# Edge tiles of 127 rows instead of 128 in a gather-and-sum graph layer on one Trainium2 core

## The chip, the cores and the metric

The kernel runs on one core of one Trainium2 chip. The metric is the device time of one execution in microseconds (us), lower is better. The kernel before takes 1381.88 us (median of two runs, 1380.68 and 1383.08).

## What is computed

`x` has 6250 nodes of 128 float32 features; 100,000 edges carry a source node, a destination node and a type 0 or 1, and come sorted by destination. Cut to what matters, the reference is:

```
Xs     = X[src]
m_data = Xs @ W_data.T + b_data
m_ctrl = Xs @ W_control.T + b_control
msg    = where(edge_types == 0, m_data, m_ctrl)
agg    = segment_sum(msg, dst, num_segments=6250)
out    = relu(agg + (X @ W_self.T + b_self))
result = layernorm(x + out)          # over the 128 features
```

## The kernel before

Nodes are padded to 49 blocks of 128 (`NB`), taken in 7 groups of 7 blocks (`GB`, `NG`). The work has a front and a long middle.

**Front.** GpSimd loads all edges once (`e_all`, L65), SyncE's queue loads weights, biases and the transposed features (`w_sb`, `bias_sb`, `xt_sb`, L67 to L72). VectorE counts, for each of 48 block borders, how many destinations lie below it (`less`, L96); one small matmul (L99) and one instruction (L101) make of it `first`, the place in the edge list at which each block's edges begin. TensorE and VectorE make both possible messages of every node, `y` (L109, L110), and ScalarE's queue writes them to a table in DRAM in seven stores of 896 KB (L111). Then (in the code; on its queue, once `first` is there) SyncE's queue reads each block's *window* of edges: `values_load` puts the window's start into a register (L119), and one DMA (L123) brings `KT * P` = 18 x 128 edges of three int32 into `win`, as 128 rows of 54 numbers (216 bytes), one row to a partition. ScalarE's queue also loads `x_sb` (L127).

**Middle.** For each group VectorE turns windows into table rows (`idx`, L132 and L133) and into destinations relative to their block (`rel`, L181), and counts the edges that lie inside (L183, L185). For each block and each of 18 tiles, GpSimd issues one indirect DMA (L195) that gathers 128 rows of 512 bytes from the table into `msg`, VectorE builds a one-hot matrix `hot` (L199), and TensorE adds `hot`^T x `msg` to `agg` in PSUM (L201; the self term L193 opened it). When a block is complete VectorE adds bias, relu and residual (L138, L139); after seven blocks the norm (L145 to L162) and one store on SyncE's queue (L166; the last, of 106 rows, L171). At the very end the count of matched edges is compared with 100,000 (L207 to L214); only if they differ, a slow loop over all edges runs. The fullest block of these inputs has 2184 edges.

**What sets the order.** The framework schedules each engine's instructions and gives every DMA one of eight completion semaphores per kind, here called lanes: eight for DMAs issued by SyncE and ScalarE together, eight for those issued by GpSimd. A DMA waits until the previous DMA on its lane has landed. In the built program, from the eighth on, a gather so waits for the gather eight before it. The lanes of SyncE and ScalarE tie the table stores to the window loads: counting windows from 0, store 3 (of 7) waits for window 5, store 4 for window 10, store 5 for window 14, store 6 for window 18, store 7 for window 23. On VectorE's queue the `idx` work of group 0 waits for windows 0 to 6 and stands in front of the later `y` additions; the next groups' `other` (L132, up to window 27) stands in front of the first block's L138. The first gather waits for the last table stores and for `idx` of group 0 (VectorE's 73rd counted instruction). Buffers: `y` and `idx` two, `msg` four blocks, `hot` three blocks, `agg` two.

Of the kernel before, what the change touches and what calls it, by code (L numbers as in the profile page):

```python
# [9 lines left out]
F32 = mybir.dt.float32  # L10
I32 = mybir.dt.int32
# [4 lines left out]
DRAM = bass.MemoryType.DRAM  # L16

P = 128
D = 128  # features
N = 6250  # nodes  # L20
E = 100000  # edges
NB = 49  # blocks of 128 nodes, the last one padded
NP = NB * P
GB = 7  # blocks in a group: one store, one set of norms
NG = NB // GB
KT = 18  # tiles of 128 edges in a block's window
WIN = KT * P
EC = 125  # edges are cut into 125 rows of 800
EPS = 1e-05


# [1 line left out]
def kernel(  # L33
    ctx: ExitStack,
    tc: tile.TileContext,
    x: bass.AP,  # [NP, D], zero rows behind N
    xt: bass.AP,  # [D, NP], its transpose
    edges: bass.AP,  # [E, 3]: source, destination, type
    w: bass.AP,  # [D, 3 * D]: data, control and self weights, transposed
    bias: bass.AP,  # [1, 3 * D]  # L40
    out: bass.AP,  # [N, D]
):
    """out = layernorm(x + relu(sum over in-edges of (W_type x_src + b_type) + W_self x + b_self))

    Both messages of each node go to a table in DRAM, at rows 2 * node + (type != 0). Edges come
    sorted by destination, so those of a block of 128 nodes lie behind one another: a window of
    WIN edges from the block's first one (found on the chip) is gathered from the table, 128 rows
    at a time, and summed by destination with one-hot matrices on the tensor engine. An edge
    outside its block matches no column there. The edges matched are counted; if any was missed
    (a block with more edges than its window, or edges in another order), a loop over all  # L50
    edges that takes them in any order does the sums again.
    """
    nc = tc.nc

    const = ctx.enter_context(tc.tile_pool(name="const", bufs=1))
    dram = ctx.enter_context(tc.tile_pool(name="dram", bufs=1, space=DRAM))
    work = ctx.enter_context(tc.tile_pool(name="work", bufs=2))
    deep = ctx.enter_context(tc.tile_pool(name="deep", bufs=4))
# [1 line left out]
    ps_a = ctx.enter_context(tc.tile_pool(name="ps_a", bufs=2, space=PSUM))  # L60
    ps_s = ctx.enter_context(tc.tile_pool(name="ps_s", bufs=1, space=PSUM))

# [1 line left out]
    e_all = const.tile([EC, E // EC, 3], I32, name="e_all")  # L64
    nc.gpsimd.dma_start(e_all, edges.rearrange("(p k) c -> p k c", p=EC))  # L65
    w_sb = const.tile([D, 3 * D], F32, name="w_sb")
# [9 lines left out]
    x_sb = const.tile([P, NB, D], F32, name="x_sb")  # L76
    x_rows = x.rearrange("(b p) f -> p b f", p=P)

# [1 line left out]
    ones = const.tile([P, 1], F32, name="ones")  # L80
    nc.vector.memset(ones, 1.0)
    slots = const.tile([P, P], F32, name="slots")
    nc.gpsimd.iota(slots, pattern=[[1, P]], base=0, channel_multiplier=0,
                   allow_small_or_imprecise_dtypes=True)
    base = const.tile([P, NB, KT], F32, name="base")
    nc.gpsimd.iota(base, pattern=[[P, NB], [0, KT]], base=0, channel_multiplier=0,
                   allow_small_or_imprecise_dtypes=True)

# [1 line left out]
    dst_f = const.tile([EC, E // EC], F32, name="dst_f")  # L90
    nc.vector.tensor_copy(dst_f, e_all[:, :, 1])  # L91
    before = const.tile([EC, NB], F32, name="before")
# [7 lines left out]
    first = const.tile([1, NB], I32, name="first")  # L100
    nc.vector.tensor_scalar_min(first, first_ps, float(E - WIN))  # L101

# [1 line left out]
    table = dram.tile([NP, 2 * D], F32, name="table")  # L104
    for g in range(NG):
        y = work.tile([P, GB, 2 * D], F32, name="y")
# [6 lines left out]
        )  # L113
    rows = table.rearrange("n (t f) -> (n t) f", t=2)

# [1 line left out]
    win = const.tile([P, NB, KT, 3], I32, name="win")  # L117
    for b in range(NB):
        at = nc.values_load(  # L119
            first[0:1, b : b + 1], engines=(SP,), min_val=0, max_val=E - WIN,  # L120
            skip_runtime_bounds_check_because="it counts edges and is held to E - WIN",
        )
        nc.sync.dma_start(  # L123
            win[:, b, :, :], edges[ds(at, WIN), :].rearrange("(p k) c -> p k c", p=P)
        )
    for g in range(NG):
        nc.scalar.dma_start(x_sb[:, g * GB : (g + 1) * GB, :], x_rows[:, g * GB : (g + 1) * GB, :])  # L127

    def table_rows(index, source, kind, shape):
        """index = 2 * source + (kind != 0)"""  # L130
        other = work.tile(shape, I32, name="other")
        nc.vector.tensor_single_scalar(other, kind, 0.0, op=ALU.not_equal)  # L132
        nc.vector.scalar_tensor_tensor(index, source, 2.0, other, op0=ALU.mult, op1=ALU.add)  # L133

    def residual(h, agg, b):
        """h = x + relu(agg + b_self)"""
        s = work.tile([P, D], F32, name="s")
        nc.vector.tensor_add(s, agg, bias_sb[:, 2 * D :])  # L138
        nc.vector.scalar_tensor_tensor(h, s, 0.0, x_sb[:, b, :], op0=ALU.max, op1=ALU.add)  # L139

    def norm_and_store(h, g):
        mv = work.tile([P, GB, 2], F32, name="mv")
        for j in range(GB):
            st = work.tile([P, 6], F32, name="st")
            nc.vector.bn_stats(st, h[:, j, :])  # L145
            nc.vector.bn_aggr(mv[:, j, :], st)  # L146
        # One step of Newton's method behind the table's square root: 1 / root is 2 / (s + v / s).
        v = work.tile([P, GB], F32, name="v")
        nc.vector.tensor_scalar_add(v, mv[:, :, 1], EPS)  # L149
        s0 = work.tile([P, GB], F32, name="s0")  # L150
        nc.scalar.activation(s0, v, AF.Sqrt)  # L151
        r0 = work.tile([P, GB], F32, name="r0")
        nc.vector.reciprocal(r0, s0)
        q = work.tile([P, GB], F32, name="q")
        nc.vector.tensor_mul(q, v, r0)
        nc.vector.tensor_add(q, q, s0)
        rstd = work.tile([P, GB], F32, name="rstd")
        nc.vector.reciprocal(rstd, q)
        nc.vector.tensor_scalar_mul(rstd, rstd, 2.0)
        o = work.tile([P, GB, D], F32, name="o")  # L160
        for j in range(GB):
            nc.vector.tensor_scalar(o[:, j, :], h[:, j, :], mv[:, j, 0:1], rstd[:, j : j + 1],  # L162
                                    op0=ALU.subtract, op1=ALU.mult)
        n0 = g * GB * P
        full = min(GB, (N - n0) // P)
        nc.sync.dma_start(  # L166
            out[n0 : n0 + full * P, :].rearrange("(b p) f -> p b f", p=P), o[:, :full, :]
        )
        if full < GB:
            n1 = n0 + full * P  # L170
            nc.sync.dma_start(out[n1:N, :], o[: N - n1, full, :])  # L171

# [1 line left out]
    counts = const.tile([P, NG], F32, name="counts")  # L174
    for g in range(NG):
        gs = slice(g * GB, (g + 1) * GB)
        shape = [P, GB, KT]
        idx = work.tile(shape, I32, name="idx")
        table_rows(idx, win[:, gs, :, 0], win[:, gs, :, 2], shape)
        rel = work.tile(shape, F32, name="rel")  # L180
        nc.vector.tensor_sub(rel, win[:, gs, :, 1], base[:, gs, :])  # L181
        low = work.tile(shape, F32, name="low")
        nc.vector.tensor_single_scalar(low, rel, float(P), op=ALU.is_lt)  # L183
        inside = work.tile(shape, F32, name="inside")
        nc.vector.scalar_tensor_tensor(inside, rel, 0.0, low, op0=ALU.is_ge, op1=ALU.mult,  # L185
                                       accum_out=counts[:, g : g + 1])
        h = work.tile([P, GB, D], F32, name="h")
        for j in range(GB):
            b = g * GB + j
            msg = deep.tile([P, KT, D], F32, name="msg")  # L190
            hot = deep.tile([P, KT, P], F32, name="hot", bufs=3)
            agg = ps_a.tile([P, D], F32, name="agg")
            nc.tensor.matmul(agg, xt_sb[:, b, :], w_sb[:, 2 * D :], start=True, stop=False)  # L193
            for k in range(KT):
                nc.gpsimd.indirect_dma_start(  # L195
                    out=msg[:, k, :], out_offset=None, in_=rows,
                    in_offset=bass.IndirectOffsetOnAxis(ap=idx[:, j, k : k + 1], axis=0),
                )
                nc.vector.tensor_single_scalar(hot[:, k, :], slots, rel[:, j, k : k + 1],  # L199
                                               op=ALU.is_equal)  # L200
                nc.tensor.matmul(agg, hot[:, k, :], msg[:, k, :], start=False, stop=k == KT - 1)  # L201
            residual(h[:, j, :], agg, b)
        norm_and_store(h, g)

# [1 line left out]
    total_ps = ps_s.tile([1, NG], F32, name="total_ps")  # L206
    nc.tensor.matmul(total_ps, ones, counts, start=True, stop=True)  # L207
    total_f = const.tile([1, 1], F32, name="total_f")
    nc.vector.tensor_reduce(total_f, total_ps, axis=mybir.AxisListType.X, op=ALU.add)
    total = const.tile([1, 1], I32, name="total")  # L210
# [1 line left out]
    matched = nc.values_load(total[0:1, 0:1])  # L212

    with tc.If(matched != E):  # L214
        # Rows behind N take what is not to be added: an edge whose destination an earlier edge of
        # its tile has already is in that edge's sum.
        sums = dram.tile([N + P, D], F32, name="sums")
        ident = const.tile([P, P], F32, name="ident")
        make_identity(nc, ident)
# [13 lines left out]
        with tc.For_i(0, E, EC) as i:  # L233
# [16 lines left out]
            n_again = work.tile([EC, 1], F32, name="n_again")  # L250
            nc.vector.scalar_tensor_tensor(again, same, 1.0, earlier[:EC, :EC], op0=ALU.mult,
                                           op1=ALU.mult, accum_out=n_again)
            # The destination, or a spare row where it came before.
            away = work.tile([EC, 1], F32, name="away")
            nc.vector.tensor_sub(away, spare[:EC], to)
            nc.vector.scalar_tensor_tensor(away, n_again, 0.0, away, op0=ALU.is_gt, op1=ALU.mult)
# [54 lines left out]
```

## Time and profile before

| what | value |
|---|---|
| time, median of 2 runs (lowest, highest) | 1381.88 us (1380.68, 1383.08) |
| span of the profiled execution (first to last instruction) | 1220.6 us |
| time of the runs less that span (the profile lists no other time of its own execution) | 161.3 us |
| first gather starts / last gather starts | 98.12 us / 1206.64 us |
| GpSimd busy | 843.7 us, 69% of the span |
| TensorE matmul busy | 747.0 us, 61% |
| VectorE busy | 305.0 us, 25% |
| DMA moved | 77.32 MB in 55893 packets, mean 63 GB/s |
| granted TensorE clock, mean | 0.540 |

How to read it: PE, PEld, DVE, ACT, POOL and SP are TensorE matmul, TensorE weight load, VectorE, ScalarE, GpSimd and SyncE; a q behind the name (SPq, ACTq) is that engine's DMA-issuing queue. A group of the profile names line, engine, operation and tiles (out<-in), shapes and count, then busy time and the mean length of one in ns, then the idle time ahead of it and what ended most of it. In the DMA lists, the last number is the median time from issue to landing. "issue" is time in which an engine waited for nothing that the profile shows. A POOL bar of an indirect DMA ends before its data has landed.

### The profile page before, as it was taken

Reading aid. Unit: us, or ns where it says so; the run is one execution under the profiler, and the core shown is the slowest. Engines: PE = TensorE matmul, PEld = TensorE weight load, DVE = VectorE, ACT = ScalarE, POOL = GpSimd, SP = SyncE. Lnnn points to the kernel's source line nnn. Section 1 sums busy time; section 2 is a strip of 40 time slices with the busy share of each in tenths; the row PEclk is TensorE's granted clock in tenths of the full one; section 3 lists DMA queues with packets and bytes.
Section 4 is the critical chain, followed back from the end, with each engine's and each line's share of the span. In section 5 each row is a group of like instructions: output and inputs, shape, how many; then the busy total and the mean of one; then the engine's idle time right before and its main releaser. Section 6 shows DMA issues by size and latency. Waiting matters only on the chain.

```text
span 1220.6 us, 6620 instructions
## 1 busy us (share of the span) xinstructions
PE 747.0 (61%) x1964; PEld 478.7 (39%) x1964; DVE 305.0 (25%) x1362; ACT 2.7 (0%) x8; POOL 843.7 (69%) x889
## 2 busy tenths in 40 slices
PE   1094666666666666666666666666666666666664
PEld 0042444444444344444444444444444444444442
DVE  4982211221212312212213113113122112212101
ACT  0000000000000000000000000000000000000000
POOL 0005777777777777777777777777777777777774
PEclk9995555555555555555555555555555555555555
DMA  8063121122212211121222212222122211221121
GB/s 263 0 200 95 52 54 52 52 67 54 52 52 52 69 52 52 52 54 52 67 54 53 52 52 67 54 52 53 52 67 54 52 52 52 68 53 52 52 54 49
DMA packets 55893, 77.32 MB, mean 63 GB/s; under 512 B 21669, under 2 KB 40719, under 8 KB 55727
## 3 DMA queue, kind: packets, MB, share of 16 engines
q0 software_dynamic: 28368, 59.06, 18.6%
q1 hardware_dynamic: 14716, 8.16, 2.5%
q10 hardware_dynamic: 12768, 9.63, 2.4%
q8 instruction: 16, 0.26, 0.1%
q14 instruction: 25, 0.20, 0.1%
HBM read 67.17 MB, written 9.62 MB: 63 GB/s over the span
## 4 chain that ended last, share of the span: by engine, by line
POOL 63%; issue 23%; DMA 5%; DVE 5%; PE 2%; POOLq 0%; SPq 0%; DVEq 0%; ACT 0%; ACTq 0%
POOL msg L195 63%; DMA msg<-table,idx 4%; DVE less L96 4%; PE y_ps L109 2%; DMA xt_sb<-in_xt 1%; DVE hot L199 1%; DVE y L110 1%; PE agg L201 0%; DVE o L162 0%; POOLq L307 0%; SPq L67 0%; SPq L69 0%; POOLq L195 0%; PE first_ps L99 0%; DVE other L132 0%
## 5 line engine op out<-in xcount | busy, mean ns | idle before, releaser
L195 POOL DMA_INDIRECT msg<-table,idx x882 | 840.9, 953 | 362.6 <-issue 259.5
L201 PE MATMUL agg<-msg,hot 128*128 128x128 f32 x1764 | 695.2, 500 | 403.0 <-DMA msg<-table,idx 400.7
L201 PEld LDWEIGHTS agg<-msg,hot 128*128 128x128 f32 x1764 | 441.0, 311 | 656.5 <-DMA msg<-table,idx 656.2
L138 DVE TENSOR_TENSOR s<-agg,bias_sb 128x128 f32<-128x128 f32 x49 | 14.3, 292 | 790.4 <-PE agg L201 790.4
L199 DVE TENSOR_SCALAR hot<-slots,rel 128x128 f32<-128x128 f32 x882 | 189.0, 292 | 0.0
L96 DVE TENSOR_SCALAR_CACHE_REDUCE less<-dst_f 125x800 f32<-125x800 f32 x48 | 43.6, 980 | 0.0
L109 PE MATMUL y_ps<-w_sb,xt_sb 128*128 128x256 f32 x98 | 31.4, 449 | 18.5 <-DMA xt_sb<-in_xt 16.8
L193 PE MATMUL agg<-w_sb,xt_sb 128*128 128x128 f32 x98 | 31.2, 423 | 0.0
L109 PEld LDWEIGHTS y_ps<-w_sb,xt_sb 128*128 128x128 f32 x98 | 16.5, 207 | 31.9 <-issue 16.8
L193 PEld LDWEIGHTS agg<-w_sb,xt_sb 128*128 128x128 f32 x98 | 27.0, 333 | 0.6 <-DVE s L138 0.3
L99 PE MATMUL first_ps<-before,ones 125*1 125x49 f32 x2 | 0.3, 260 | 41.5 <-DVE less L96 41.5
L133 DVE SCALAR_TENSOR_TENSOR idx<-win,other 128x126 int32<-128x126 int32 x7 | 2.3, 324 | 88.0 <-DMA msg<-table,idx 88.0
L110 DVE TENSOR_TENSOR y<-y_ps,bias_sb 128x256 f32<-128x256 f32 x49 | 20.5, 424 | 5.0 <-PE y_ps L109 3.8
L99 PEld LDWEIGHTS first_ps<-before,ones 125*1 125x1 f32 x2 | 0.1, 80 | 41.8 <-DVE less L96 41.8
L139 DVE SCALAR_TENSOR_TENSOR h<-s,x_sb 128x128 f32<-128x128 f32 x49 | 14.5, 295 | 0.1
L145 DVE BATCH_NORM_STATS2 st<-h 128x6 f32<-128x128 f32 x49 | 13.7, 280 | 0.1
L162 DVE TENSOR_SCALAR o<-h,mv,rstd 128x128 f32<-128x128 f32 x49 | 13.5, 363 | 0.0
L146 DVE BATCH_NORM_AGGREGATE mv<-st 128x2 f32<-128x6 f32 x49 | 8.6, 176 | 0.9
L91 DVE CAST dst_f<-e_all 125x800 f32<-125x800 int32 x1 | 0.7, 693 | 15.5 <-DMA e_all<-in_edges 15.5
L151 ACT ACTIVATE s<-v 128x7 f32<-128x7 f32 x7 | 1.5, 208 | 1115.5 <-DVE v L149 1115.5
L96 DVE DVE_READ_ACCUMULATOR less<-dst_f 125x1 f32 x48 | 3.9, 82 | 0.0
L181 DVE TENSOR_TENSOR rel<-win,base 128x126 f32<-128x126 int32 x7 | 2.1, 305 | 0.0
(25 smaller groups left out, 19.2 us busy)
## 6 DMA issues: line engine op xcount, KB each, us to landing
msg<-table,idx POOLq DMA_INDIRECT x882, 2.5
table<-y ACTq DMA_DIRECT2D x7, 896.0 KB, 4.2
x_sb<-in_x ACTq DMA_DIRECT2D x7, 448.0 KB, 14.6
xt_sb<-in_xt SPq DMA_DIRECT2D x7, 448.0 KB, 10.4
out<-o SPq DMA_DIRECT2D x6, 448.0 KB, 3.0
win<-in_edges SPq DMA_DIRECT2D x49, 27.0 KB, 1.9
e_all<-in_edges POOLq DMA_DIRECT2D x1, 1171.9 KB, 15.2
out<-o SPq DMA_DIRECT2D x1, 384.0 KB, 3.4
```

The source lines that it names most:

```text
L96: nc.vector.tensor_scalar(less, dst_f, float(b * P), None, op0=ALU.is_lt, op1=ALU.add, accum_out=before[:, b : b + 1])
L109: nc.tensor.matmul(y_ps, xt_sb[:, g * GB + j, :], w_sb[:, : 2 * D], start=True, stop=True)
L110: nc.vector.tensor_add(y[:, j, :], y_ps, bias_sb[:, : 2 * D])
L138: nc.vector.tensor_add(s, agg, bias_sb[:, 2 * D :])
L139: nc.vector.scalar_tensor_tensor(h, s, 0.0, x_sb[:, b, :], op0=ALU.max, op1=ALU.add)
L145: nc.vector.bn_stats(st, h[:, j, :])
L146: nc.vector.bn_aggr(mv[:, j, :], st)
L162: nc.vector.tensor_scalar(o[:, j, :], h[:, j, :], mv[:, j, 0:1], rstd[:, j : j + 1], op0=ALU.subtract, op1=ALU.mult)
L193: nc.tensor.matmul(agg, xt_sb[:, b, :], w_sb[:, 2 * D :], start=True, stop=False)
L195: nc.gpsimd.indirect_dma_start(out=msg[:, k, :], out_offset=None, in_=rows, in_offset=bass.IndirectOffsetOnAxis(ap=idx[:, j, k : k + 1], a ...
L199: nc.vector.tensor_single_scalar(hot[:, k, :], slots, rel[:, j, k : k + 1], op=ALU.is_equal)
L201: nc.tensor.matmul(agg, hot[:, k, :], msg[:, k, :], start=False, stop=k == KT - 1)
```

## The change

A constant `R = 127` takes the place of 128 for the number of edges in a tile. Everything that has one partition per edge has 127 partitions: the window (2286 edges instead of 2304, still 18 edges to a row), `idx`, `rel`, `msg`, `hot`, and each of the 882 gathers. The number of tiles stays 18 per block, so no instruction is added or removed: on all five engines the instructions, their order and the semaphores they wait for are the same in both built programs, with 127 in the place of 128. Blocks of nodes, the message table, the norms and the stores keep 128. Comments are taken out.

```diff
 KT = 18
-WIN = KT * P
+R = 127
+WIN = KT * R
...
-    win = const.tile([P, NB, KT, 3], I32, name="win")
+    win = const.tile([R, NB, KT, 3], I32, name="win")
...
-            win[:, b, :, :], edges[ds(at, WIN), :].rearrange("(p k) c -> p k c", p=P)
+            win[:, b, :, :], edges[ds(at, WIN), :].rearrange("(p k) c -> p k c", p=R)
...
-        shape = [P, GB, KT]
+        shape = [R, GB, KT]
...
-        nc.vector.tensor_sub(rel, win[:, gs, :, 1], base[:, gs, :])
+        nc.vector.tensor_sub(rel, win[:, gs, :, 1], base[:R, gs, :])
...
-                                       accum_out=counts[:, g : g + 1])
+                                       accum_out=counts[:R, g : g + 1])
...
-            msg = deep.tile([P, KT, D], F32, name="msg")
-            hot = deep.tile([P, KT, P], F32, name="hot", bufs=3)
+            msg = deep.tile([R, KT, D], F32, name="msg")
+            hot = deep.tile([R, KT, P], F32, name="hot", bufs=3)
...
-                nc.vector.tensor_single_scalar(hot[:, k, :], slots, rel[:, j, k : k + 1],
+                nc.vector.tensor_single_scalar(hot[:, k, :], slots[:R], rel[:, j, k : k + 1],
                                                op=ALU.is_equal)
...
-    nc.tensor.matmul(total_ps, ones, counts, start=True, stop=True)
+    nc.tensor.matmul(total_ps, ones[:R], counts[:R], start=True, stop=True)
```

## The prediction, made blind

> **What bounds the kernel now.** I read the chain of waits first, then the groups by line, then the timeline around the first gather, then the DMA issues. Chain and groups:
>
> ```profile
> POOL 63%; issue 23%; DMA 5%; DVE 5%; PE 2%; POOLq 0%; SPq 0%; DVEq 0%; ACT 0%; ACTq 0%
> ...
> L195 POOL DMA_INDIRECT msg<-table,idx x882 | 840.9, 953 | 362.6 <-issue 259.5
> L201 PE MATMUL agg<-msg,hot 128*128 128x128 f32 x1764 | 695.2, 500 | 403.0 <-DMA msg<-table,idx 400.7
> ```
>
> See: the chain is GpSimd issuing gathers, with "issue" (no visible wait) between them, while TensorE waits 400.7 us for gathered rows. The first gather starts at 98.12 us and the 882nd at 1206.64 us, so the pace is 1108.5 / 881 = 1.258 us. TensorE needs about 0.80 us per tile (the timeline's two matmuls of a tile) and VectorE 0.21 us; both follow. So the time has three terms: the front up to 98.1 us, 882 x 1.258 us, and a tail of 14 us; 161.3 us lie around the span (1381.88 - 1220.6), and I leave them alone. The timeline shows what ends the front:
>
> ```profile
> 63.47 49.07 SPq L123 DMA_DIRECT2D win<-in_edges  x49
> ...
> 66.51 26.87 ACTq L111 DMA_DIRECT2D table<-y  x7
> ...
> 98.12 1.03 POOL L195 DMA_INDIRECT msg<-table,idx  x1 [94.01 <-DVE inside L185]
> 99.45 0.96 POOL L195 DMA_INDIRECT msg<-table,idx  x1 [0.30 <-issue]
> ```
>
> and the DMA issues:
>
> ```profile
> msg<-table,idx POOLq DMA_INDIRECT x882, 2.5
> table<-y ACTq DMA_DIRECT2D x7, 896.0 KB, 4.2
> ...
> win<-in_edges SPq DMA_DIRECT2D x49, 27.0 KB, 1.9
> ```
>
> See: SyncE issues a window load per 1.00 us (49.07 / 49), each landing after 1.9 us; store 7 of the table is issued at 93.0 us and lands 4.2 us later, and the gathers then start. The profile names VectorE's L185 as releaser, but the built program only waits there for `idx` of group 0 (done near 73 us), so I take the store as the real release.
>
> [...] In its packet records (size, time and duration of each DMA packet), the last store of 106 rows (divisor 2) drains as two interleaved streams, each a 512-byte row per 23.4 ns, so the divisor counts on SyncE's queue. The 125-row `e_all` load of GpSimd moved up to 20 packets per us of 601 ns each, at least 12 engines' worth, so that direct copy isn't confined to 5. No run here shows an indirect gather with an odd row count. [...]
>
> **The change part by part.** The built program has the same instructions, order and waits on all engines; only lengths can change.
>
> *Window loads (49).* 127 rows of 216 bytes would all go to one engine, always the same one. The packet records give 16 ns as the median of such a row (mean 19.7 with waits), so one load takes that engine 127 x 16 = 2.03 us, where 16 engines took 0.13 us each. The loads now queue at 2.04 us instead of 1.00 us. On the same engine lies its share of each table store: 56 rows of 1 KB at 46 ns = 2.6 us. Store 7 waits on its lane for window 23, the 24th load. That lands at 63.5 + (1.9 - 0.13) + 24 x 2.04 + 6 stores x 2.6 = 129.8 us. Store 7 was issued at 93.0 us; so it is late by 36.8 us. Its own rows on that engine alternate with queued window rows: 56 x 16 ns = 0.9 us more. First gather: 98.1 + 37.7 = 135.8 us.
>
> Is something else later still? VectorE stops at `idx` of group 0 until window 6: 63.5 + 1.8 + 7 x 2.04 + 2 x 2.6 = 84.8 us instead of 71.8 us, 13 us late. Behind it stand `y` additions and `hot`; the last `y` addition moves from 92.8 to 106 us, or some 10 us more where stores 4 to 6 wait for windows 10, 14 and 18: by about 116 us, before 129.8. VectorE's `other` for window 27 ends near 139 us; behind it L138 of block 0 is wanted only at 136 + 18 x 1.26 = 158 us. Later windows (all landed by about 185 us) serve groups that start 158 us apart. These cost nothing under that cover; at 24 ns per row (the spacing of the last store), the 24 loads cost 24 us more and the cover for L138 still nearly holds. Bounds for this term: 0 (spread) to 62 us (24 ns); I take 37.7, since packet time is what one engine can pass.
>
> *Gather, data.* 127 rows on one engine are 16 packets of up to 4096 bytes. A packet took 229 ns (median; 156 and 382 at the 5th and 95th percentile), so the last row lands 15 x 0.229 = 3.4 us later: 5.9 us instead of 2.5. The wait this meets is the lane: gather i waits for gather i-8, that is 8 x 1.258 = 10.1 us. 5.9 is under it[...]. So nothing on the pace; 3.4 us once, at the last gather, since the tail waits for it. Bounds: 0 (spread over 16) to 5.7 us (382 ns).
>
> *Gather, generation.* 127 rows instead of 128: if all 953 ns are per row, 7.4 ns x 882 = 6.6 us less; if none, 0. I take 3.3. Whether one ring is dearer or cheaper to fill than sixteen shows nowhere in this trace: 1% of the 840.9 us is 8.4 us. I take zero for it and treat it as cases below.
>
> *Compute.* Matmul contraction and the DVE tiles lose one partition of 128; [...] both engines wait anyway: 0. The fullest block, 2184 edges, fits 2286, so the slow loop stays out.
>
> Sum: 37.7 + 3.4 - 3.3 = +37.8 us. Span 1258.4, time 1381.9 + 37.8 = 1420 us (median and span are set together by the constant 161.3).
>
> **The rivals.**
>
> *A, likeliest (45%).* As summed. Own range 1405 (14 ns rows, gathers spread, full saving of 6.6) to 1450 (24 ns rows, slow gather packets).
>
> *B, generation gets dearer (22%).* [...] For it: POOL is the pace, so everything counts 882 times. Against: no row shows it. +10% is 84 us, 1504; +25% is 210 us, 1630.
>
> *C, generation gets cheaper, the other side (18%).* If much of the 953 ns is work per DMA engine[...], a gather on one ring saves some of it at L195. Against: [...]the packet records show 16 four-byte packets per gather[...]. It decides at 37.8 / 840.9 = 4.5%: more saving than that ends below the time before. At 10%: 1420 - 84 = 1336.
>
> *D, gathers in one line (6%).* [...]every gather sits on the same engine: 16 x 0.229 = 3.7 us per gather, the lane wait binds, 882 x (3.7 - 1.26) = 2150 us more, about 3570 us. The same wait decides whenever landing passes 10.1 us, 60 ns per row; the trace's 29 ns per row[...] speak against it.
>
> *E, the change doesn't do that (9%).* Windows spread over 16 engines as `e_all` did, gathers too. Then only the row less counts: 1382 - 3 = 1378 us. The two streams of the 106-row store speak against it.
>
> **How the numbers follow.** The time is A's, 1420. A measurement of this kernel tells about 2% (27.6 us) from no change: below 1354 is faster, above 1409.5 slower. Slower: four fifths of A (0.37), B (0.22), D (0.06) = 0.65. Faster: C where it saves over 8% (0.10), 0.11 with a rest. Same: the remainder of A and C, and E, 0.24. For the range I leave out D, the worst fourth of B (above 1560) and the lower half of C (below 1350): 0.06 + 0.06 + 0.09 = 0.21. So 1350 to 1560, and 1405 to 1450 for A alone.
>
> **What would show it.** In the profile after: window loads to landing well above 1.9 us, up to 14 us when seven queue; the window line of SyncE's queue about 100 us or more long; store 7 near 130 us; the first gather near 136 us; gathers to landing near 5.9 us; GpSimd's mean 947 to 953 ns; idle before L195 still "issue" 0.30 us. Wrong in A: first gather below 110 us (windows spread, or one engine passes rows faster than 16 ns), POOL's mean off by over 2% (B or C), or gathers waiting for gathers (D).

## The result and the profile after

The changed kernel takes 2660.93 us (median of two runs, 2660.41 and 2661.45) where the kernel before takes 1381.88 us: a ratio of 1.926, 95% interval 1.920 to 1.931. The forecast was 1420 us with a range up to 1560; it is missed by far. The profiled execution has a span of 2658.2 us, and its own time is 2660.4 us, so only 2.2 us lie around the span.

The kernel before runs at one of two speeds according to the chip, 1375 to 1383 us on some and 1220 to 1222 us on another, and the profile of before (span 1220.6 us) shows the second, as run 7 below confirms. So the "161.3 us" that "lie around the span" don't exist, and each experiment below is compared with runs of the kernel before on its own chip.

First the page of the changed kernel: the chain's shares by engine, then the two groups (busy us, mean ns | idle us before them and what ended most of it). Every line number is one higher than before.

```profile
POOL 79%; issue 10%; DMA 7%; DVE 2%; SPq 2%; PE 1%; POOLq 0%; DVEq 0%; ACT 0%; ACTq 0%
...
L196 POOL DMA_INDIRECT msg<-table,idx x882 | 2246.2, 2547 | 391.5 <-issue 385.7
L202 PE MATMUL agg<-msg,hot 127*128 127x128 f32 x1764 | 701.7, 501 | 1815.2 <-DMA msg<-table,idx 1815.2
```

See: the same chain as before, GpSimd issuing gathers, and the same count of them. Only the length of one has changed, from 953 to 2547 ns. TensorE's matmuls are as long as they were (501 ns) and wait 1815.2 us for rows.

The timeline around the first gather (start and length in us):

```profile
63.61 108.37 SPq L124 DMA_DIRECT2D win<-in_edges  x49
...
66.52 53.77 ACTq L112 DMA_DIRECT2D table<-y  x7
...
127.26 2.62 POOL L196 DMA_INDIRECT msg<-table,idx  x1 [123.14 <-issue]
```

See: the window loads take 108.37 us instead of 49.07 us, 2.2 us each; the last table store is issued near 120 us instead of 93; and the first gather starts at 127.26 us instead of 98.12. The gap ahead of a gather is still 0.30 us of "issue". A gather's line in the DMA issues ends with the time from issue to landing:

```profile
msg<-table,idx POOLq DMA_INDIRECT x882, 7.7
```

The span's difference, term by term: the front 127.26 - 98.12 = 29.1 us; the pace, (2639.26 - 127.26) / 881 = 2.851 us per gather instead of 1.258, so 881 x 1.593 = 1403.4 us; the tail from the start of the last gather 18.9 us instead of 14.0, so 5.0 us. 1220.6 + 29.1 + 1403.4 + 5.0 = 2658.1, the span but for rounding. Nearly all of it is the length of one instruction.

What is in those 1.6 us shows in a part of the page that I hadn't used in the forecast, the DMA queues (packets, MB, share of 16 engines). GpSimd's queue q0, first before, then after:

```profile
q0 software_dynamic: 28368, 59.06, 18.6%
```

```profile
q0 software_dynamic: 240048, 65.33, 15.4%
```

Before: 28368 = 144 (the one load of all edges) + 882 x 32, and 32 is 16 packets of eight 512-byte rows and 16 marks of four bytes. After: (240048 - 144) / 882 = 272, that is 240 packets more for the same rows. The bytes say what they are. 882 x 127 x 512 B are 57.35 MB, the load of the edges 1.20 MB, the marks 0.06 MB; 6.72 MB are left, 7620 bytes per gather, which is 15 x 127 x 4. The packet records of the trace agree: per gather they hold 15 packets of 4096 bytes and one of 3584 (127 rows, eight to a packet), 16 of four bytes, 225 of 32 bytes and 15 of 28. 225 and 15 are fifteen times the same, 15 packets of 32 bytes and one of 28, in four-byte pieces 15 x 8 + 7 = 127. The records carry no engine number, but one reading meets all these counts, and those of six other row counts below: the 127 rows are one share of a gather, and fifteen further shares of 127 four-byte fillers each go with it, as many as the one share has rows.

### The profile page after: what moved, and what is told of

The parts are those of the page before. It is cut to its first block, busy times and chain, and to the rows that moved or that the text cites. A ratio compares the mean times of both kernels' runs of the same rounds, so it can differ in the third digit from the quotient of the medians.

```text
span 2658.2 us, 6620 instructions
## 1 busy us (share of the span) xinstructions
PE 757.1 (28%) x1964; PEld 481.9 (18%) x1964; DVE 542.4 (20%) x1362; ACT 2.7 (0%) x8; POOL 2249.1 (85%) x889
## 3 DMA queue, kind: packets, MB, share of 16 engines
q0 software_dynamic: 240048, 65.33, 15.4%
q1 hardware_dynamic: 13932, 8.15, 1.1%
## 4 chain that ended last, share of the span: by engine, by line
POOL 79%; issue 10%; DMA 7%; DVE 2%; SPq 2%; PE 1%; POOLq 0%; DVEq 0%; ACT 0%; ACTq 0%
POOL msg L196 79%; DMA msg<-table,idx 6%; DVE less L97 2%; SPq L124 1%; SPq L120 1%; DMA xt_sb<-in_xt 1%; PE agg L202 1%; DMA table<-y 0%; DMA win<-in_edges 0%; POOLq L308 0%; DVE o L163 0%; PE y_ps L110 0%; DVE y L111 0%; SPq L70 0%; SPq L68 0%
## 5 line engine op out<-in xcount | busy, mean ns | idle before, releaser
L196 POOL DMA_INDIRECT msg<-table,idx x882 | 2246.2, 2547 | 391.5 <-issue 385.7
L202 PE MATMUL agg<-msg,hot 127*128 127x128 f32 x1764 | 701.7, 501 | 1815.2 <-DMA msg<-table,idx 1815.2
L202 PEld LDWEIGHTS agg<-msg,hot 127*128 127x128 f32 x1764 | 441.8, 311 | 2075.0 <-DMA msg<-table,idx 2075.0
L200 DVE TENSOR_SCALAR hot<-slots,rel 127x128 f32<-127x128 f32 x882 | 409.9, 786 | 0.0
L139 DVE TENSOR_TENSOR s<-agg,bias_sb 128x128 f32<-128x128 f32 x49 | 14.3, 292 | 1830.0 <-PE agg L202 1829.9
L146 DVE BATCH_NORM_STATS2 st<-h 128x6 f32<-128x128 f32 x49 | 31.6, 644 | 0.1
L163 DVE TENSOR_SCALAR o<-h,mv,rstd 128x128 f32<-128x128 f32 x49 | 25.0, 782 | 0.0
L140 DVE SCALAR_TENSOR_TENSOR h<-s,x_sb 128x128 f32<-128x128 f32 x49 | 21.7, 444 | 0.1
L184 DVE TENSOR_SCALAR low<-rel 127x126 f32<-127x126 f32 x7 | 9.6, 1367 | 0.0
```

The source lines that it names most:

```text
L196: nc.gpsimd.indirect_dma_start(out=msg[:, k, :], out_offset=None, in_=rows, in_offset=bass.IndirectOffsetOnAxis(ap=idx[:, j, k : k + 1], a ...
L200: nc.vector.tensor_single_scalar(hot[:, k, :], slots[:R], rel[:, j, k : k + 1], op=ALU.is_equal)
```

## The experiments

**Theory 1.** It carries the reading of the packet counts on to other row counts. Let k be the largest divisor of the row count up to 16, and r the rows divided by k. Theory 1 has the rows of a gather in k shares of r rows, has fillers make up 16 shares where k is below 16, and lets the time of the instruction on GpSimd grow with r. That k is what decides was my assumption before these runs; the table below holds it against the counts. The recorded texts call a share a ring, so r is the rows of the fullest ring. The first two points (r = 8 at 128 rows, 127 at 127) give 846 ns + 13.4 ns x r.

**Rivals.** Any row count other than a multiple of 16 takes a slow path of one price (2547 ns). Or the common divisor with 16 alone decides (125 like 127, 126 like 122). Or the new time comes from the windows. Or GpSimd is held up by the rows' transfer, which takes longer in one share (rival 4). Or the price goes by packets and not by r; no run was made for this one, but runs 4 and 6 together decide it. Runs 1 to 4, 5 to 8 and 9 to 12 were made on one chip each, on which the kernel before took 1376.4, 1220.87 and 1376.08 us.

**1. Windows of 127 rows, gathers of 128.** Windows, `rel` and `hot` keep 127 rows, only the gathers go back; the index of partition 127 is zero and its row is gathered but not summed.

```diff
-        idx = work.tile(shape, I32, name="idx")
-        table_rows(idx, win[:, gs, :, 0], win[:, gs, :, 2], shape)
+        idx = work.tile([P, GB, KT], I32, name="idx")
+        nc.vector.memset(idx, 0)
+        table_rows(idx[:R], win[:, gs, :, 0], win[:, gs, :, 2], shape)
...
-            msg = deep.tile([R, KT, D], F32, name="msg")
+            msg = deep.tile([P, KT, D], F32, name="msg")
...
-                nc.tensor.matmul(agg, hot[:, k, :], msg[:, k, :], start=False, stop=k == KT - 1)
+                nc.tensor.matmul(agg, hot[:, k, :], msg[:R, k, :], start=False, stop=k == KT - 1)
```

> Windows stay at 127 rows, but each gather has 128: the 128th row's index is a constant 0 and its row is left out of the matmul, so the result is unchanged. Theory 1 (the loss sits in the generation of a 127-row gather): GpSimd's mean goes back to 953 ns and the pace to 1.26 us; only the front stays late by the window loads, first gather at 127 us, time 29 us above the kernel before. Rival (windows, lanes or the odd tile width slow the middle too): the pace stays well above 1.26 us and the time hundreds of us above the kernel before.

Measured: 1404.59 us, ratio 1.020 (1.019 to 1.022), 28 us above before. The gather line of the source view (minimum / median / maximum ns, first and last start):

```profile
L197 POOL DMA_INDIRECT msg<-table,idx x882: 938/944/1126, 128.1 to 1371.2; - x177
```

So the front is worth the windows' 29 us and nothing else, and the gathers' length isn't the windows' doing. The pace, (1371.2 - 128.1) / 881 = 1.411 us, misses the expected 1.26. The windows can't be the reason: 0.153 us more per gather than 1.258 would cost 135 us over the kernel before, and 28 us were measured. It is the slower chips' second limit, taken up below.

**2. The opposite: windows in two loads of 112 and 15 rows, gathers of 127.**

```diff
-        nc.sync.dma_start(
-            win[:, b, :, :], edges[ds(at, WIN), :].rearrange("(p k) c -> p k c", p=R)
-        )
+        src = edges[ds(at, WIN), :].rearrange("(p k) c -> p k c", p=R)
+        nc.sync.dma_start(win[:112, b, :, :], src[:112])
+        nc.sync.dma_start(win[112:, b, :, :], src[112:])
```

> The mirror of it: gathers stay at 127 rows, each window is loaded as two DMAs of 112 and 15 rows, which divide by 16 and 15. Theory 1: first gather back to 100 to 115 us (98 of the kernel before, and up to 15 more since there are 49 more DMAs to issue), generation stays at 2547 ns, span 2658 less 12 to 29 us. Rival: if the windows' single DMA engine also drives the slow generation, the pace falls.

Measured: 2636.72 us (one run).

```profile
L196 POOL DMA_INDIRECT msg<-table,idx x882: 2537/2542/2623, 102.0 to 2614.9; - x177
```

The first gather is back at 102.0 us, 25.3 us earlier than in the changed kernel, and the time is about as much lower (24 us against the 2660.93 us above, 21 us against run 12). The gathers' shortest, median and longest are the same to the nanosecond. Windows and gathers add up and don't act on each other.

**3 and 4. Row counts with other divisors: 126 (k = 14, r = 9) and 122 (k = 2, r = 61).** Edit: `R = 126` and `R = 122`; 18 tiles still hold the fullest block (18 x 122 = 2196 edges, 2184 needed).

> All tiles 126 rows, whose largest divisor up to 16 is 14: 9 rows to a ring. Theory 1 ([...]13.4 ns per row of a ring: (2547 - 953) / (127 - 8)): 953 + 13.4 x 1 = 966 ns, pace 1.27 us, first gather near 98 us, time within 2% of the kernel before. Rival 2 (any number of rings but 16 is one slow path): about 2547 ns. Rival 3 (what counts is the common divisor with 16, here 2, so 63 rows to a ring): 953 + 13.4 x 55 = 1690 ns.

> All tiles 122 rows, divisor 2: 61 rows to a ring. Theory 1: 953 + 13.4 x 53 = 1663 ns, pace 1.97 us, so 881 x 0.71 = 623 us more than the kernel before in the middle; in the packet records about 14 of 16 rings get filler packets. Rival 2 (one slow path): 2547 ns. Rival 3 gives the same as theory 1 here. Window loads use 2 engines, 61 x 16 ns = 1.0 us each, no longer than their issue: first gather 98 to 110 us.

Measured: 126 rows 1379.62 us, ratio 1.0017 (1.0009 to 1.0025); 122 rows 1857.76 us (one run). The group's line and q0 of 126, then of 122:

```profile
L196 POOL DMA_INDIRECT msg<-table,idx x882: 982/987/1203, 101.1 to 1345.5; - x177
```

```profile
q0 software_dynamic: 42480, 58.22, 16.4%
```

```profile
L196 POOL DMA_INDIRECT msg<-table,idx x882: 1652/1659/1804, 106.6 to 1839.0; - x177
```

```profile
q0 software_dynamic: 127152, 59.36, 16.6%
```

The slow path of one price falls at once: 126 isn't a multiple of 16 and costs 987 ns. So does the divisor of 16 alone: 126 and 122 share the same 2 with 16 and differ by 672 ns. 122 lands on Theory 1 (mean 1662, expected 1663). 126 lies 28 ns above it (mean 994, expected 966). That its time came out within 2% of the kernel before, as expected, is in part luck: the pace is 1.412 us and not 1.27, so this chip's second limit sets the time and not the gather. The packets follow: 48 per gather at 126, as the reading has it (28 of rows, 16 marks, and two for each of two shares of fillers), and 144 at 122 (16, 16, and eight for each of fourteen).

**5. 125 rows (k = 5, r = 25), with no divisor in common with 16, as 127.** Edit: `R = 125`.

> All tiles 125 rows: no common divisor with 16, but divisor 5. Theory 1 ([...]a line through the two longest points is 846 + 13.4 ns per row of a ring): 25 rows to a ring, 846 + 335 = 1181 ns, perhaps 30 ns more as the 126-row tiles had. Rival 3 (common divisor with 16): all 125 rows in one ring, 846 + 1675 = 2521 ns. Rival 2 (one slow path for anything but 16 rings): fell with the run before and is not expected.

Measured: 1449.36 us (one run), before 1220.87 us.

```profile
L196 POOL DMA_INDIRECT msg<-table,idx x882: 1195/1200/1412, 101.5 to 1432.6; - x177
```

Having no common divisor with 16 isn't what counts: 125 has none either, and its gather takes 1200 ns where that with 127 takes 2542. What tells the two apart here is k, 5 for 125 and 1 for 127, which has no divisor from 2 to 16 at all. On this chip nothing hides the price: 882 x (1206 - 953) ns are 223 us, the front is 3 us later, and the time is 228 us above before.

**6. 127 rows of half the bytes.** The second half of the features is left out.

```diff
+    halves = table.rearrange("n (t f) -> (n t) f", t=4)
...
+        nc.vector.tensor_add(idx, idx, idx)
...
-                    out=msg[:, k, :], out_offset=None, in_=rows,
+                    out=msg[:, k, : D // 2], out_offset=None, in_=halves,
...
-                nc.tensor.matmul(agg, hot[:, k, :], msg[:, k, :], start=False, stop=k == KT - 1)
+                nc.tensor.matmul(agg[:, : D // 2], hot[:, k, :], msg[:, k, : D // 2], start=False, stop=k == KT - 1)
```

> The changed kernel, but each gathered row is 256 bytes instead of 512: the second half of the features of all messages is left out of the gathers and the matmuls. Theory 1[...]: GpSimd's mean stays at 2547 ns within 1%, the time at 2661 us within 1%; only the landing falls, by about half of the 3.6 us that one engine needs for 127 rows, from 7.7 to about 6 us. Rival 4[...]: the mean falls with the data time, by 1 us or more, to 1.5 us or less.

Measured: 2656.09 us (one run). Source view, then DMA issues, then q0:

```profile
L198 POOL DMA_INDIRECT msg<-table,idx x882: 2534/2539/2621, 127.5 to 2637.1; - x177
```

```profile
msg<-table,idx POOLq DMA_INDIRECT x882, 5.8
```

```profile
q0 software_dynamic: 127152, 36.65, 31.9%
```

Half the bytes land 1.9 us earlier (5.8 us after the issue instead of 7.7), and GpSimd takes 3 ns less. So GpSimd doesn't wait for the rows' transfer: rival 4 falls. The fillers' bytes are as many as before (36.65 MB on q0 is 28.68 of rows, 6.72 of fillers, 1.26 of the rest). But the packets are nearly halved, 144 per gather instead of 272, which is what sixteen rows or fillers to a packet give instead of eight. These are the packets of run 4, whose gather takes 1659 ns and not 2539. So the price follows r (61 there, 127 here) and not the packets.

**7 and 8. The kernel before again, and with more buffers.** The pace of run 1 and the time of the kernel before on the slower chips raised the question whether TensorE and VectorE wait for buffers. The second of these kernels has four `agg` and four `hot` buffers; small PSUM tiles share space to make room.

```diff
-    ps_a = ctx.enter_context(tc.tile_pool(name="ps_a", bufs=2, space=PSUM))
+    ps_a = ctx.enter_context(tc.tile_pool(name="ps_a", bufs=4, space=PSUM))
...
-            hot = deep.tile([P, KT, P], F32, name="hot", bufs=3)
+            hot = deep.tile([P, KT, P], F32, name="hot", bufs=4)
```

> The kernel before, profiled once more: the profile shown of it has a span of 1220.6 us while its runs take 1376 to 1383 us. If that profile is typical and some 160 us lie around the span, the span is 1220 us again. If its own execution went differently from the timed ones, the span is about 1375 us, and the difference stands as stalls of GpSimd at the end of every second block, about 6 us each (24 x 6.2 us), as in the kernel with 127-row windows and 128-row gathers; the mean of a gather stays 947 to 953 ns either way.

> The kernel before with four accumulators in PSUM instead of two and four buffers of hot matrices instead of three. In the profile of the kernel with 128-row gathers TensorE stands about 32 us of every 51 us waiting for an accumulator, and GpSimd then runs out of msg buffers for 6 us. If the depth of that handshake is what costs the kernel before its 155 us over the 1220 us of its profile, the time falls to 1225 to 1300 us; if whatever holds the handshake back is not a matter of depth, it stays at 1376 us within 1%.

Measured: 1220.95 us, and 1221.8 us with more buffers, ratio 1.0006 (0.9997 to 1.0015). Both ran on the chip where the kernel before takes 1221 us and GpSimd has no wait but its own 0.30 us, so buffers could gain nothing. For the slower chips this settles nothing. The profile of the first gives the gather 952 ns once more, and its span (1218.9) is 2.0 us below its own time: that is how the supposed 161.3 us fell.

**9. 112 rows (k = 16, r = 7, no fillers), 20 tiles to a block.** Edit: `R = 112`, `KT = 20`.

> Tiles of 112 edges, 20 to a block instead of 18 (980 gathers instead of 882): k = 16, 7 rows to a ring, no fillers. Theory 1 as it stands (time by the rows of the fullest ring, 846 + 13.4 ns each): GpSimd's mean 940 ns, so 980 x (0.940 + 0.305) = 1220 us of gathers where the kernel before has 882 x 1.257 = 1109 us, the time about 111 us above the kernel before; 32 packets per gather or fewer, no small ones beside the marks. Rival (only fillers cost time, real rows nothing): 953 ns, 1233 us, about 124 us above. Rival (an odd multiple of 16 rows is dear too): over 1000 ns, at least 170 us above.

Measured: 1519.66 us, ratio 1.104 (1.102 to 1.106).

```profile
L196 POOL DMA_INDIRECT msg<-table,idx x980 | 919.9, 939 | 558.6 <-issue 279.1
```

The mean is 939 ns as Theory 1 had it (940) and not 953, so the rival that only fillers cost time falls, if by 14 ns alone. q0 has 31504 = 144 + 980 x 32 packets: at 7 x 16 rows, as at 8 x 16, there are no fillers, and one row more in each of the 16 shares costs 11 to 14 ns (medians 933 at r = 7, 944 to 947 at r = 8). The time is 144 us above before, not 111: the idle time ahead of the gathers grew too. The waits of GpSimd, in us in total, times and longest:

```profile
POOL msg L196 <- issue: 279.1, 916, 0.3
POOL msg L196 <- remote: 173.1, 24, 16.8
```

173.1 us in 24 waits for something whose release the trace doesn't hold ("remote"). This is the slower chips' second limit, taken up below.

**10. 124 rows (k = 4, r = 31).** Edit: `R = 124`.

> Tiles of 124 edges: k = 4, 31 rows to a ring, 12 rings of fillers. Theory 1: 846 + 13.4 x 31 = 1261 ns; 80 packets of the gather queue per gather (16 of data, 16 marks, 48 of fillers); 882 x (1.261 + 0.305) = 1381 us of gathers, the span near 1500 us. Where the excess of 25 to 28 ns of the runs with 126 and 125 rows over the line belongs to every row count with fillers: 1287 ns. The rival that any count other than a multiple of 16 is equally dear: 2547 ns, span near 2640 us.

Measured: 1526.89 us (one run).

```profile
L196 POOL DMA_INDIRECT msg<-table,idx x882 | 1140.7, 1293 | 366.3 <-issue 258.6
```

1293 ns; the line alone wants 1261, with the excess of 126 and 125 rows 1287. So three counts with fillers lie 25 to 32 ns above the line of Theory 1. 122 rows doesn't (1662 against 1663), and 127 rows is the line's own end. A line that runs from a count without fillers to one with them is the wrong one, and that 122 met it within 1 ns is luck; the table below draws it anew.

**11. 126 rows again, to see its 41 ns per gather in the time.** 

> The tiles of 126 edges once more, beside the kernel before of this call. If the kernel before shows about 1221 us here, so no idle time of GpSimd hides anything, Theory 1 wants the 41 ns that a gather took longer at 126 rows in full: 882 x 0.041 = 36 us, and some 3 us of the front, so about 1257 to 1261 us. If the rival holds that 41 ns a gather costs nothing even then: 1221 us. If the kernel before shows about 1376 us here, about 1379 us again.

Measured: 1381.87 us, ratio 1.0043 (1.0026 to 1.0059); mean 993 ns. The kernel before took 1376.08 us on this chip, so the case with no other waits didn't come up. GpSimd's "remote" waits are 100.2 us here and in run 3, and 147.0 us in run 1 with its shorter gathers: idle time takes the 36 us in. Whether 126 rows cost 36 us on a chip of the faster sort wasn't measured.

**12. The changed kernel again.**

> The changed kernel once more, beside the kernel before of this call. Theory 1: GpSimd's mean 2547 ns again and 2660 us again, whether the kernel before shows 1221 us or 1380 us in this call, because a GpSimd that is busy 2.55 us of 2.85 us leaves nothing late behind it: a ratio of 2.18 in the first case, 1.93 in the second.

Measured: 2657.92 us, ratio 1.931 (1.927 to 1.935); mean 2545 ns. It wasn't run beside a kernel before of 1221 us; run 6, which differs from it by 3 ns a gather, was, and took 2656.09 us there, 2.18 times 1220.87.

**All counts together.** Median of one gather, packets of q0 and of SyncE's queue q1 as the page has them:

| rows | k | r = rows / k | median ns | q0 packets | q1 packets |
|---|---|---|---|---|---|
| 112 | 16 | 7 | 933 | 31504 (980 gathers) | 13932 |
| 128 | 16 | 8 | 947 | 28368 | 14716 |
| 126 | 14 | 9 | 987 | 42480 | 14520 |
| 125 | 5 | 25 | 1200 | 70704 | 14030 |
| 124 | 4 | 31 | 1292 | 70704 | 13932 |
| 122 | 2 | 61 | 1659 | 127152 | 13736 |
| 127 | 1 | 127 | 2542 | 240048 | 13932 |

Every number of q0 is 144 + gathers x (16 + 16 x r / 8 rounded up): 16 marks, and 16 times the packets of one share, eight rows to a packet. Every number of q1 is 7660 + 49 x (rows + k): a window load has one packet per row and k marks. (The records of q1 hold 1042 packets of four bytes before and 307 after, 49 x 15 fewer.) Both hold to the packet in seven kernels. Run 2 fits too (loads of 112 and 15 rows: 7660 + 49 x (112 + 16 + 15 + 15) = 15402, which its page shows). For the time, 868 + 13.2 x r ns meets the five counts with fillers within 15 ns; the two without lie 27 ns below that line. Theory 1 holds with this correction: a price of some 27 ns where there are fillers at all. That it is fixed isn't shown: 124 rows lie 15 ns above the line and 122 rows 14 below, while repeats of a count agree within 3 ns, so something small is left over.

## Why the prediction was wrong

*What bounds the kernel.* Right: it still is GpSimd issuing gathers, and everything counts 882 times.

*Window loads.* The idea was right, and the size high: 29.1 us instead of 37.7. k = 1 is shown by q1's count. That all rows pass one after another fits the packet records: of the gaps between the starts of window rows 5673 of 6271 were below 10 ns before, and none of 6222 is after (median 13 ns). A load takes 2.2 us instead of the forecast 2.04. Store 7 is issued near 120 us, not at 129.8. The term that was too large is the stores' share. In the packet records the rows of windows 0, 24 and 48 begin at 64.5, 119.5 and 173.3 us: 2.29 us per load while the stores pass, 2.24 after them. By this pace the six stores added about 1 us (24 x 0.05, an estimate) and not 15.6, and each load is 0.2 us dearer than forecast. The gaps between row starts tell more: mostly 13 ns, they make 1.65 us of a load's 2.2. Before window 24, 240 of 3048 gaps lie between 40 and 70 ns (median 55), as with one of the stores' 1 KB rows (46 ns) between, some 10 us in all (240 x 42 ns, an estimate). In as many gaps after it 63 do, but those above 70 ns sum to 9.6 us instead of 4.9; what they wait for isn't shown. Nothing else was later, as forecast.

*Gather, data.* Right. The landing is 7.7 us and not 5.9, but 1.6 us of that are the longer instruction; after GpSimd's bar ends the data takes 7.7 - 2.55 = 5.15 us instead of 2.5 - 0.95 = 1.55, so 3.6 us more where 3.4 were forecast. The wait on the gather eight before never binds: GpSimd waits for a gather 0.3 us in all.

*Gather, generation.* This is the step that failed: "Whether one ring is dearer or cheaper to fill than sixteen shows nowhere in this trace [...] I take zero for it and treat it as cases below." It costs 1.594 us per gather, 1403 us. Rival B had the place and the sign, but its sizes, 10 and 25%, came from nowhere; it is 167%. Over the seven row counts the price goes by r, about 13 ns for each unit of it, and B had no such measure. That a transfer has k shares was an assumption of the forecast, for which the forecast had one place in the trace of before, the two streams of the 106-row store. The packet counts of seven row counts now bear it out on both queues, and the 16 marks per gather stay at all of them. Fillers stood nowhere in the forecast; they are 240 of the 272 packets of a 127-row gather.

What the trace of before could have given is a bound: if all of the 953 ns went by r, 127 instead of 8, a gather would take 15 us (953 ns x 127 / 8, an estimate). I bounded this cost from neither side by anything measured, and the range ended at a made-up 25% where r grows sixteen times.

*The constant.* "161.3 us lie around the span [...] and I leave them alone" failed as well. In the changed kernel and all twelve experiments the time of the profiled execution exceeds its span by 1.7 to 2.2 us. By that, the 1381.88 us and the span of 1220.6 us belong to chips of different speed, so the sum had a start of 1220.6 for one sort and an unseen one for the other. By spans the change costs 1437.6 us; by the runs shown 1279 us, because on those chips the kernel before already waits for something that the longer gathers hide (the second limit below). One slip among the chances changes nothing: four fifths of A's 45% are 0.36, not 0.37.

*Rivals.* C (cheaper) fell with the mean. D (gathers in line behind one another) fell: landing stays at 7.7 us, 8.7 at most, and only one of 882 gathers waits for another, 0.3 us. E (change does nothing) fell with q0 and q1.

## What to carry to other kernels

Keep the partitions of an indirect gather at a multiple of 16, and where that isn't possible take a count whose largest divisor k up to 16 is large: in these runs the instruction took 933 and 947 ns at 112 and 128 rows, 987 at 126 and 2542 at 127, about 13 ns for each unit of rows / k on top of some 850 ns. Read the packets and bytes of a DMA queue: divided by the number of transfers they gave the shares and the fillers here, before any time was explained. And compare a profile's span with the time of its own execution before a remainder is carried along as a constant; an unknown price that counts 882 times needs a bound from something counted, not a few per cent either way.

## What the runs showed of the hardware

**Beside long gathers on GpSimd VectorE's instructions get longer; the cause is open.** VectorE's one-hot instructions (`hot`), the same work per instruction but for one partition, and one of the norm's, in the groups of before and after:

```profile
L199 DVE TENSOR_SCALAR hot<-slots,rel 128x128 f32<-128x128 f32 x882 | 189.0, 292 | 0.0
...
L145 DVE BATCH_NORM_STATS2 st<-h 128x6 f32<-128x128 f32 x49 | 13.7, 280 | 0.1
```

```profile
L200 DVE TENSOR_SCALAR hot<-slots,rel 127x128 f32<-127x128 f32 x882 | 409.9, 786 | 0.0
...
L146 DVE BATCH_NORM_STATS2 st<-h 128x6 f32<-128x128 f32 x49 | 31.6, 644 | 0.1
```

And `hot` in the source view after:

```profile
L200 DVE TENSOR_SCALAR hot<-slots,rel x882: 232/279/2092, 85.2 to 2502.6; 127x128 f32<-127x128 f32 x177
```

The median is 279 ns (278 with 128 rows, run 7), and the longest takes 2092 ns, not quite one gather's 2547. The mean of `hot` grows with that of the gather: 292 ns at 953, 346 at 1206, 390 at 1293, 509 at 1662, 786 at 2547. BATCH_NORM_STATS2 and a RECIPROCAL get longer too, from 280 to 644 ns and from 197 to 615 in the mean, while the addition at L138 (now L139) keeps its 292 ns. So few long ones stand among many short, and not of one form alone; no run here separates one cause from another. It costs nothing here, since VectorE waits anyway (1829.9 us for sums on TensorE).

**A second limit of 1.41 us per tile on the slower chips, open.** The four profiles from such chips whose GpSimd needs less than that per tile (runs 1, 3, 9, 11: 1.254, 1.299, 1.244 and 1.298 us with the gap) all have the same pace from first to last gather: 1.411, 1.412, 1.413 and 1.412 us. It holds for 18 and for 20 tiles to a block, so it belongs to the tile. Where GpSimd needs more (1.60 us in run 10, 1.97 in run 4, 2.85 in runs 2 and 12) it isn't seen. So 126 rows seem free there and 112 rows cost 33 us more than forecast; and it accounts for the 155 us between the runs of before on the two sorts of chip (881 x (1.411 - 1.258) = 135 us, and a tail of 32 us instead of 14 in run 1). The clock granted to TensorE isn't lower there, 0.614 in the mean in run 11 against 0.540 in run 7. TensorE's timeline of run 11 has bursts, and between them single records:

```profile
412.23 5.43 PE L202 MATMUL agg<-msg,hot 126*128 126x128 f32 x30
418.31 0.27 PE L202 MATMUL agg<-msg,hot 126*128 126x128 f32 x1 [0.65 <-issue]
421.11 0.27 PE L202 MATMUL agg<-msg,hot 126*128 126x128 f32 x1 [2.53 <-issue]
424.61 0.37 PE L202 MATMUL agg<-msg,hot 126*128 126x128 f32 x1 [3.23 <-DMA msg<-table,idx]
426.71 0.37 PE L202 MATMUL agg<-msg,hot 126*128 126x128 f32 x1 [1.73 <-issue]
429.51 0.37 PE L202 MATMUL agg<-msg,hot 126*128 126x128 f32 x1 [2.43 <-issue]
432.31 0.37 PE L202 MATMUL agg<-msg,hot 126*128 126x128 f32 x1 [2.43 <-issue]
```

After thirty matmuls in 5.43 us the starts lie 2.80, 3.50, 2.10, 2.80 and 2.80 us apart, multiples of 0.70 us. A TensorE that takes 0.70 us per matmul would need 1.40 us per tile, which fits the pace. But the same view shows thirty in 5.43 us, 0.18 us each, and with the six single ones the 36 of a block are complete, so a TensorE that always needs 0.70 us isn't what it shows. That TensorE is the limit there is argued and not shown, and why it would be slower on one chip than on another stays open.
